# Scans and maxima with one operand in PSUM, and a reordered tail, in a two-layer graph network kernel

## The chip, the cores and the metric

The kernel runs on one core of one Trainium2 chip. The metric is device microseconds of one execution; the median of several runs counts. All inputs start in HBM and the result has to be back there.

## The reference

A graph of N = 6250 nodes with 128 features and E = 100000 edges, sorted by destination. Two layers, each followed by a residual and a layernorm. The first layer sums messages `relu(W·[x[src], edge])` per destination. The second, which the change touches, is an attention layer with 4 heads of 32 channels:

```python
xl = (x @ w_l + b_l).reshape(N, H, C)
xr = (x @ w_r + b_r).reshape(N, H, C)
e = leaky_relu(xl[src] + xr[dst], 0.2)          # every node has an edge to itself too
logits = einsum('ehc,hc->eh', e, att)
m = segment_max(logits, dst, num_segments=N)
ex = exp(logits - m[dst])
alpha = ex / segment_sum(ex, dst)[dst]
out = segment_sum(xl[src] * alpha[:, :, None], dst).reshape(N, H * C) + bias
out = (out - out.mean()) / (out.std() + 1e-5)   # over the whole array
x = layernorm(x + out * ln_w + ln_b)
```

## The kernel before

**Tiling.** Nodes lie in 49 blocks of 128. Edges lie in 784 tiles of 128, four tiles (512 edges) to a group, GN = 196 groups. The program runs in stages: node projections and index tables; layer 1 over the groups; layer 2 over the groups (1321 to 2697 us of the profile); a final stage with the global mean and deviation and the last layernorm, seven groups of BG = 7 blocks each, about 38 us. A second version of the layers, `far`, is for graphs that are not sorted well enough and is not entered here.

**Layer 2** is one loop over steps s, its order written out by hand, with no scheduler. A step issues, in this order:

- `gather_group(s + 4)`: four indirect DMAs by GpSimd (L262), each 128 rows of `xl_t` into a ring of 30 groups (`XG`). A slot of the ring is free once `values` of its group is done.
- on SyncE's queue, `store_sums` of groups that were summed in the step before (L1005, `out_t<-win`), loads `m_load` (`dm`) and `out_load` (L1010, `s<-out_t`), and `load_rows` (`xr`, `ds`). A store adds nothing: it writes a window of 128 consecutive destination rows at a row number read at run time, and windows may overlap, so stores, and the loads of the same table, follow each other in order.
- `copy_both(s-1)` (ACT, L818, `z<-pz`), `both(s)` (PE, L811 transposes of the gathered rows and L814 the destination rows, into `pz`), `leaky(s-1)` (DVE, L821), `logits(s-2)` (PE, L840, into `plg`), `onehot_t(s+1)` (ACT, L804).
- `sums(u)` for the groups u due in step s (PE, L985: one-hot `a` times values `v`, into the window `pa`) and `keep_sums` (ACT, L1001, `win`).
- for the groups due in the next step: `values_w` (ACT, L969), `values` (DVE, L973, gathered rows times weights, into `v`), and the one-hot of destinations (DVE, L579, `a`).
- what a plan lists for that step: parts of the softmax chain and of the outputs.

**The chain.** Logits of twelve groups (a macro: 15 of twelve, then 9 and 7) stand as 48 rows (head, group) of 512 in PSUM, `plg`. One macro's chain goes through six steps: `m_logits` copies `plg` to SBUF (ACT, L857, `lg`) and makes `pen`, -BIG where a new destination starts (DVE, L860 and L861); `m_forward` and `m_back` take running maxima within a destination with scans (L865, L869); `m_ends`, `m_groups`, `m_before` carry maxima over from group to group (PE, small DVE operations on one partition, PE); `m_maxima` makes each edge's maximum `mx` from the scans and carried values (`fp` L922, L924), then `lg - mx` (L926), and ACT exponentiates; `m_weights`, `m_left`, `m_ready` turn the weights back to edges on partitions. The PSUM bank `pw` is one buffer, handed from use to use in that order. `m_logits` stands at the front of its step (list `FIRST`), the others at its end. Two groups of values are due per step from step 166 on, one before.

**Outputs.** Once all windows of a block are stored, `out_load` brings its sums back from `out_t`, `out_weights` (L1019 to L1026, the first operation writes `m0`) weighs them against the node's own edge, and `output` (L1034 to L1042) normalises them and adds the own edge. Its last part, `ready`, takes bn statistics of the block and multiplies `xl` by `ln_w` (L259). Blocks go by twos, the last few singly, and the last three (46 to 48) together. Load, weights and output are planned 1, 4 and 5 steps after the step in which the last store's group is summed.

The head of the loop shows how gathers, stores and the front of the plan stand to each other:

```python
for s in range(stop + 1):
    if s + AHEAD < GN:
        gather_group(s + AHEAD, xl_t)
    for u in due.get(s - 1, ()):
        store_sums(u)
    planned(s, only=FIRST)
```

Of the kernel before, what the change touches and what calls it, by code (L numbers as in the profile page):

```python
# [9 lines left out]
F32 = mybir.dt.float32  # L10
# [72 lines left out]
def gnn_resnorm(  # L83
# [165 lines left out]
    def ready(pool, b0, n):  # L249


        bs = slice(b0, b0 + n)
        st = pool.tile([P, n, nc.vector.BN_STATS_DIM], F32, name=f"rd_st{n}")
        for b in range(n + 1):
            if b < n:
                nc.vector.bn_stats(st[:, b, :], xl[:, b0 + b, :])
            if b > 0:
                nc.vector.bn_aggr(stat[:, b0 + b - 1, :], st[:, b - 1, :])
        nc.vector.tensor_tensor(xl[:, bs, :], xl[:, bs, :], over(lnw_b, n), op=OP.mult)  # L259
# [294 lines left out]
    def near():  # L554
        ctx = ExitStack()
        with ctx:
# [24 lines left out]

            def first_row(g):
# [192 lines left out]
            with tc.tile_pool(name="e1", bufs=3) as pool, tc.tile_pool(name="e1m", bufs=2) as mp, \  # L775
# [79 lines left out]
                def m_logits(m):  # L855
                    m.lg = mp.tile([m.R, S], F32, name="lg")
                    nc.scalar.copy(m.lg, m.plg)  # L857
# [5 lines left out]
                def m_forward(m):  # L863
                    m.fw = mp.tile([m.R, S], F32, name="fw", bufs=1)
                    nc.vector.tensor_tensor_scan(m.fw, m.pen[:, 0:S], m.lg, -BIG, op0=OP.add, op1=OP.max)  # L865

                def m_back(m):
                    m.sm = mp.tile([m.R, S], F32, name="sm", bufs=1)
                    nc.vector.tensor_tensor_scan(m.sm[:, ::-1], m.pen[:, S:0:-1], m.fw[:, ::-1], -BIG,  # L869
                                                 op0=OP.add, op1=OP.max)  # L870

                    m.ends = mp.tile([m.R, 2], F32, name="ends")
# [5 lines left out]
                def m_ends(m):  # L878
                    m.pe = ps1.tile([P, S], F32, name="pw")
                    for i, t in enumerate((m.ends[:, 0:1], m.fw[:, S - 1:S], m.ends[:, 1:2], m.sm[:, 0:1])):  # L880
# [32 lines left out]
                def m_maxima(m):  # L913
# [4 lines left out]
                    m.mx = mp.tile([R, S], F32, name="mx")  # L918
                    for k, most in ((0, m.sm), (1, m.mx)):
                        fp = mp.tile([R, S], F32, name="fp", bufs=1)  # L920
# [5 lines left out]
                    nc.vector.tensor_sub(m.lg, m.lg, m.mx)  # L926
# [86 lines left out]
                def out_weights(b0, n):  # L1013
# [5 lines left out]
                    nc.vector.tensor_scalar(m0, s[:, :, :, 0], 0.5, -BIG, op0=OP.is_lt, op1=OP.mult)  # L1019
                    nc.vector.tensor_add(m0, m0, s[:, :, :, 1])  # L1020
                    mm = pool.tile([P, n, H], F32, name=f"mm{n}")
                    nc.vector.tensor_tensor(mm, lself[:, bs, :], m0, op=OP.max)
                    f = pool.tile([P, 2, n, H], F32, name=f"f{n}")
# [3 lines left out]
                    OUTS[b0] = s, f  # L1027

                def output(b0, n):
# [4 lines left out]
                    nc.vector.tensor_tensor(den, s[:, :, :, 0], f[:, 0], op=OP.mult)  # L1034
                    nc.vector.tensor_add(den, den, f[:, 1])
                    nc.vector.reciprocal(den, den)
                    nc.vector.tensor_tensor(f, f, den.unsqueeze(1).to_broadcast([P, 2, n, H]), op=OP.mult)
                    xh = xl[:, bs, :].rearrange("p b (h c) -> p b h c", h=H)
# [4 lines left out]
                    ready(pool, b0, n)  # L1043
# [10 lines left out]
                def planned(s, only=None, but=()):  # L1054
                    for f, of_what in at.get(s, ()):
                        if f not in but and (only is None or f in only):
                            f(*of_what)

# [18 lines left out]
                stop = max(when.values())  # L1077
                b = 0
                while b < NB - last:
                    n = 2 if b + 2 <= NB - last - 4 else 1  # L1080
                    s = when[FINAL[b + n - 1]] + 1
                    for i, f in ((1, out_load), (4, out_weights), (5, output)):
                        plan(s + i, f, b, n)
                    stop = max(stop, s + 5)
                    b += n
                stop += 1
                for i, f in enumerate((out_load, out_weights, output)):
                    plan(when[GN - 1] + 1 if i == 0 else stop, f, NB - last, last)
# [7 lines left out]
                FIRST = (m_load, out_load, m_logits)  # L1096
                for s in range(stop + 1):
# [20 lines left out]
                    for u in due.get(s + 1, ()):  # L1118
                        values_w(u)
                        values(u)  # L1120
                        OH[u] = onehot(pool, u, F32)
                    planned(s, but=FIRST)
# [285 lines left out]
```

## Time and profile before

| | us |
|---|---|
| median of 7 runs (lowest to highest) | 2748.42 (2733.93 to 2757.9) |
| the profiled execution's own time | 2737.26 |
| its span, first to last instruction | 2735.5 |
| GpSimd busy (1574 instructions) | 1507.8, 55% |
| PE busy (6269) | 1538.9, 56% |
| VectorE busy (2990) | 1216.9, 44% |
| ACT busy (1543) | 691.9, 25% |
| mean granted TensorE clock | 0.739 of full speed |

Busy time counts an engine's instructions only, not the issuing of DMAs nor waits. Shares are means over stages that have different limits; GpSimd's 782 gathers of layer 2 (`ring<-xl_t`) and 722 of layer 1 are nearly all of its time. Rows of the costliest groups read: line, engine, operation, result and operands, how many, then busy us and mean ns of one, then idle time just ahead of them and what ended most of it. In a timeline a row is start, duration, engine, line, operation, and in brackets the idle time ahead of it and what ended it.

### The profile page before, as it was taken

What the parts mean: (1) busy time and instruction counts of PE and PEld (TensorE: products, weight loads), DVE (VectorE), ACT (ScalarE), POOL (GpSimd) and SP (SyncE); (2) the same over time, 40 slices, a digit from 0 to 9 for tenths busy, and PEclk for the clock granted to TensorE, in tenths of its full rate; (3) what the DMA queues carried; (4) which work ended last, traced back from release to release, by engine and by line L of the source; (5) the groups of instructions that cost most, each with busy time, mean ns of one, the idle gap of its engine ahead of it and who ended that gap; (6) DMA issues with size and microseconds to landing.
All of it is one profiled execution on the core that took longest, in us unless ns stands there. A gap on an engine that the chain in (4) does not pass through costs nothing. (4 is left out here: it accounts for less than half of the span.)

```text
span 2735.5 us, 23587 instructions
## 1 busy us (share of the span) xinstructions
PE 1538.9 (56%) x6269; PEld 932.7 (34%) x6269; DVE 1216.9 (44%) x2990; ACT 691.9 (25%) x1543; POOL 1507.8 (55%) x1574
## 2 busy tenths in 40 slices
PE   2423544434444544467423877776777776766684
PEld 1223433333333333345101333333333333333342
DVE  2401343334444445489201534453444454455488
ACT  0101211111111111122102423333333333333333
POOL 7175666666666666620573566666665565664300
PEclk7666766676676677778656877887877787888787
DMA  4231333333333233332322323332333333333212
GB/s 116 79 82 49 70 73 71 77 70 77 76 83 81 70 87 85 85 79 62 93 61 63 100 77 95 94 98 89 91 99 89 92 104 92 98 97 92 84 43 62
DMA packets 252495, 224.66 MB, mean 82 GB/s; under 512 B 134793, under 2 KB 213751, under 8 KB 252354
## 3 DMA queue, kind: packets, MB, share of 16 engines
q1 hardware_dynamic: 201088, 120.00, 15.4%
q0 software_dynamic: 50048, 102.60, 14.9%
q8 instruction: 53, 0.87, 0.1%
q14 instruction: 88, 0.72, 0.1%
q10 hardware_dynamic: 1218, 0.47, 0.1%
HBM read 198.37 MB, written 24.56 MB: 81 GB/s over the span
## 5 line engine op out<-in xcount | busy, mean ns | idle before, releaser
L262 POOL DMA_INDIRECT ring<-xl_t,src_i x782 | 762.9, 976 | 612.8 <-issue 228.3
L262 POOL DMA_INDIRECT ring<-xw_t,src_i x722 | 684.1, 948 | 466.8 <-issue 195.0
L821 DVE SCALAR_TENSOR_TENSOR z<-z,pz 128x512 f32<-128x512 f32 x196 | 134.2, 685 | 677.9 <-ACT z L818 357.7
L985 PE MATMUL pa<-v,a 128*128 128x136 f32 x1568 | 280.1, 322 | 160.2 <-issue 81.3
L616 PE MATMUL pt<-ident,ef 128*128 128x128 f32 x392 | 102.0, 352 | 452.2 <-ACT fT L620 269.2
L985 PEld LDWEIGHTS pa<-v,a 128*128 128x128 f32 x1568 | 230.8, 216 | 333.7 <-issue 212.9
L579 DVE TENSOR_TENSOR a<-rows_q,dl 128x512 fp32r<-128x512 f32 (+1 forms) x392 | 267.0, 681 | 22.2 <-remote 17.7
L635 PE MATMUL ph<-wc,fT 128*128 128x256 f32 x784 | 267.3, 475 | 7.2 <-DVE msg L653 7.2
L653 DVE SCALAR_TENSOR_TENSOR msg<-ph,msg 128x512 fp32r<-128x512 f32 x196 | 134.8, 688 | 298.2 <-ACT msg L649 209.3
L814 PE MATMUL pz<-ds,xr 128*128 128x512 f32 x392 | 248.5, 720 | 3.6 <-issue 3.4
L840 PE MATMUL plg<-z,attw 128*48 128x512 f32 (+2 forms) x392 | 240.9, 696 | 13.3 <-issue 13.1
L811 PE MATMUL pz<-ident,ring 128*128 128x128 f32 x784 | 152.9, 323 | 151.7 <-issue 108.9
L616 PEld LDWEIGHTS pt<-ident,ef 128*128 128x128 f32 x392 | 60.4, 176 | 506.8 <-ACT fT L620 291.2
L818 ACT COPY z<-pz 128x512 f32<-128x512 f32 x196 | 114.2, 583 | 393.1 <-remote 230.3
L649 ACT ACTIVATE msg<-ph 128x512 fp32r<-128x512 f32 x196 | 117.6, 600 | 353.6 <-remote 160.3
L644 DVE TENSOR_TENSOR ph<-ph,ring 128x512 f32<-128x512 f32 x181 | 125.7, 695 | 175.4 <-remote 151.5
L620 ACT COPY fT<-pt 128x256 f32<-128x256 f32 x196 | 72.6, 370 | 484.1 <-remote 364.5
L635 PEld LDWEIGHTS ph<-wc,fT 128*128 128x128 f32 x784 | 174.1, 243 | 45.3 <-issue 11.7
L663 PE MATMUL pa<-msg,a 128*128 128x258 f32 x784 | 183.6, 369 | 0.0
L811 PEld LDWEIGHTS pz<-ident,ring 128*128 128x128 f32 x784 | 101.8, 161 | 201.3 <-issue 145.0
L973 DVE TENSOR_TENSOR v<-ring,rows_q 128x512 f32<-128x512 f32 x196 | 133.1, 679 | 59.2 <-remote 53.1
L804 ACT ACTIVATE ds<-ds,nb 128x512 f32<-128x512 f32 x196 | 142.4, 727 | 12.3 <-DMA ds<-dpad 12.3
(219 smaller groups left out, 1614.7 us busy)
## 6 DMA issues: line engine op xcount, KB each, us to landing
ds<-dpad SPq DMA_DIRECT2D x98, 512.0 KB
ef<-in_edge_attr_dram SPq DMA_DIRECT2D x48, 512.0 KB
ring<-xl_t,src_i POOLq DMA_INDIRECT x782
ring<-xw_t,src_i POOLq DMA_INDIRECT x722
out_t<-win SPq DMA_DIRECT2D x81, 68.0 KB
sum_t<-win SPq DMA_DIRECT2D x81, 64.5 KB
xr<-xr_t SPq DMA_DIRECT2D x81, 64.0 KB
xw_t<-xw SPq DMA_DIRECT2D x7, 448.0 KB
```

The lines of the kernel that those rows point to most:

```text
L262: nc.gpsimd.indirect_dma_start(out=to, out_offset=None, in_=table[0:min(table.shape[0], NP), :], in_offset=bass.IndirectOffsetOnAxis(ap=in ...
L579: nc.vector.tensor_tensor(a, over(iota_q, G), spread(dl[:, g * G:(g + 1) * G], W), op=OP.is_equal)
L616: nc.tensor.transpose(pt[:, g % 2, i, :], EF[c][:, o + 2 * i:o + 2 * i + 2, :], ident)
L635: nc.tensor.matmul(ph[:, 2 * i:2 * i + 2, :], fT[:, i, :], wc, start=i == 0 or g >= RAW, stop=g >= RAW, skip_group_check=g < RAW)
L653: nc.vector.scalar_tensor_tensor(msg[:, :, 1, 0:D], PH.pop(g), 0.0, msg[:, :, 0, 0:D].bitcast(F32), op0=OP.max, op1=OP.subtract)
L663: nc.tensor.matmul(pa, a[:, j, :], msgs[g % 3][:, j], start=g == o and j == 0, stop=j == G - 1, skip_group_check=True)
L804: nc.scalar.activation(DS[g], DS[g], AF.Abs, bias=nb[0:W, g:g + 1])
L811: nc.tensor.matmul(pz[:, j * P:(j + 1) * P], XG[g][:, j, :], ident, is_transpose=True, start=j == 0, stop=False, skip_group_check=True)
L814: nc.tensor.matmul(pz, xr, DS.pop(g), start=False, stop=True, skip_group_check=True)
L821: nc.vector.scalar_tensor_tensor(Z[g], Z[g], SLOPE, PZ.pop(g), op0=OP.mult, op1=OP.max)
L840: nc.tensor.matmul(m.plg, attw[m.mg][:, m.mg - i:m.mg - i + m.R], Z.pop(g), start=i == 0, stop=i == m.mg - 1)
L985: nc.tensor.matmul(pa, a[:, j, :], v[:, j].rearrange("p h c -> p (h c)"), start=u == o and j == 0, stop=j == G - 1, skip_group_check=True)
```

## The change

- `m_logits` no longer copies the logits to SBUF; the forward scan reads `plg` in PSUM. `m_logits` (now only `pen`) leaves `FIRST` and stands at the end of its step.
- The forward scan writes the PSUM bank `pw` (as `m.q`), the back scan reads it there; its last column is copied to a third column of `ends` for PE.
- `fp` lies in a bank `pw` of PSUM too, and `lg` is now `plg - mx`.
- For steps s from 192 (`late`, the last gather is issued in 191) the order within a step changes: the chain first, then `values_w` of all groups due, then on GpSimd the one-hots of every second group due a step later (`onehot_g`, eight groups in all, four 128x128 instructions each, a tile of its own with two buffers), then values, VectorE's one-hots and parts of the outputs in turn. `out_weights` and `output` become generators for that.
- The outputs of blocks from `LATE` = 34 on are planned at 1, 2 and 2 steps after their last sum instead of 1, 4 and 5, and not before step 192; the loop ends at step 210 instead of 213.
- The products by `ln_w` of blocks 34 to 48 leave `ready`; GpSimd makes them after the loop in three instructions (1, 7 and 7 blocks).

```diff
@@ -246,7 +246,7 @@
         nc.vector.tensor_tensor(y, y, over(att_b, n), op=OP.mult)
         nc.vector.tensor_reduce(lself[:, bs, :], y.rearrange("p b (h c) -> p b h c", h=H), AX.X, OP.add)
 
-    def ready(pool, b0, n):
+    def ready(pool, b0, n, scaled=True):
 
 
         bs = slice(b0, b0 + n)
@@ -256,7 +256,8 @@
                 nc.vector.bn_stats(st[:, b, :], xl[:, b0 + b, :])
             if b > 0:
                 nc.vector.bn_aggr(stat[:, b0 + b - 1, :], st[:, b - 1, :])
-        nc.vector.tensor_tensor(xl[:, bs, :], xl[:, bs, :], over(lnw_b, n), op=OP.mult)
+        if scaled:
+            nc.vector.tensor_tensor(xl[:, bs, :], xl[:, bs, :], over(lnw_b, n), op=OP.mult)
 
     def gather(to, table, index, t):
         nc.gpsimd.indirect_dma_start(
@@ -579,6 +580,13 @@
                 nc.vector.tensor_tensor(a, over(iota_q, G), spread(dl[:, g * G:(g + 1) * G], W), op=OP.is_equal)
                 return a
 
+            def onehot_g(pool, g):
+
+                a = pool.tile([P, G, W], F32, name="b", bufs=2)
+                for j in range(G):
+                    nc.gpsimd.tensor_scalar(a[:, j, :], iota_w, dl[:, g * G + j:g * G + j + 1], None, op0=OP.is_equal)
+                return a
+
             def first_row(g):
                 return nc.values_load(fst[0:1, g:g + 1], engines=(SP,), min_val=0, max_val=N - 1,
                                       skip_runtime_bounds_check_because="a destination, from 0 to N - 1")
@@ -853,23 +861,22 @@
 
 
                 def m_logits(m):
-                    m.lg = mp.tile([m.R, S], F32, name="lg")
-                    nc.scalar.copy(m.lg, m.plg)
 
                     m.pen = mp.tile([m.R, S + 1], F32, name="pen")
                     nc.vector.tensor_tensor(m.pen, m.dm[:, 1:], m.dm[:, 0:S + 1], op=OP.not_equal)
                     nc.vector.tensor_scalar(m.pen, m.pen, -BIG, None, op0=OP.mult)
 
                 def m_forward(m):
-                    m.fw = mp.tile([m.R, S], F32, name="fw", bufs=1)
-                    nc.vector.tensor_tensor_scan(m.fw, m.pen[:, 0:S], m.lg, -BIG, op0=OP.add, op1=OP.max)
+                    m.q = ps1.tile([P, S], F32, name="pw")[0:m.R, :]
+                    nc.vector.tensor_tensor_scan(m.q, m.pen[:, 0:S], m.plg, -BIG, op0=OP.add, op1=OP.max)
 
                 def m_back(m):
                     m.sm = mp.tile([m.R, S], F32, name="sm", bufs=1)
-                    nc.vector.tensor_tensor_scan(m.sm[:, ::-1], m.pen[:, S:0:-1], m.fw[:, ::-1], -BIG,
+                    nc.vector.tensor_tensor_scan(m.sm[:, ::-1], m.pen[:, S:0:-1], m.q[:, ::-1], -BIG,
                                                  op0=OP.add, op1=OP.max)
 
-                    m.ends = mp.tile([m.R, 2], F32, name="ends")
+                    m.ends = mp.tile([m.R, 3], F32, name="ends")
+                    nc.vector.tensor_copy(m.ends[:, 2:3], m.q[:, S - 1:S])
                     nc.vector.tensor_scalar(m.ends[:, 0:1], m.dm[:, S:S + 1], m.dm[:, 0:1], -BIG,
                                             op0=OP.not_equal, op1=OP.mult)
                     nc.vector.tensor_scalar(m.ends[:, 1:2], m.dm[:, 1:2], m.dm[:, S + 1:S + 2], -BIG,
@@ -877,7 +884,7 @@
 
                 def m_ends(m):
                     m.pe = ps1.tile([P, S], F32, name="pw")
-                    for i, t in enumerate((m.ends[:, 0:1], m.fw[:, S - 1:S], m.ends[:, 1:2], m.sm[:, 0:1])):
+                    for i, t in enumerate((m.ends[:, 0:1], m.ends[:, 2:3], m.ends[:, 1:2], m.sm[:, 0:1])):
                         nc.tensor.transpose(m.pe[0:1, i * P:i * P + m.R], t, ident[0:m.R, 0:m.R])
 
                 def m_groups(m):
@@ -916,14 +923,15 @@
                     nc.vector.tensor_copy(prev, m.pv[0:R, 0:2])
 
                     m.mx = mp.tile([R, S], F32, name="mx")
+                    fp = ps1.tile([P, S], F32, name="pw")[0:R, :]
                     for k, most in ((0, m.sm), (1, m.mx)):
-                        fp = mp.tile([R, S], F32, name="fp", bufs=1)
                         o = k * (S + 1)
                         nc.vector.tensor_scalar(fp, m.dm[:, 1:S + 1], m.dm[:, o:o + 1], -BIG,
                                                 op0=OP.not_equal, op1=OP.mult)
                         nc.vector.scalar_tensor_tensor(m.mx, fp, prev[:, k:k + 1], most, op0=OP.add, op1=OP.max)
 
-                    nc.vector.tensor_sub(m.lg, m.lg, m.mx)
+                    m.lg = mp.tile([R, S], F32, name="lg")
+                    nc.vector.tensor_sub(m.lg, m.plg, m.mx)
                     m.sc = mp.tile([R, 1], F32, name="sc")
                     nc.vector.scalar_tensor_tensor(m.sc, m.pen[:, 0:1], prev[:, 0:1], m.mx[:, 0:1], op0=OP.add,
                                                    op1=OP.subtract)
@@ -1017,14 +1025,18 @@
 
                     m0 = pool.tile([P, n, H], F32, name=f"m0{n}")
                     nc.vector.tensor_scalar(m0, s[:, :, :, 0], 0.5, -BIG, op0=OP.is_lt, op1=OP.mult)
+                    yield
                     nc.vector.tensor_add(m0, m0, s[:, :, :, 1])
+                    yield
                     mm = pool.tile([P, n, H], F32, name=f"mm{n}")
                     nc.vector.tensor_tensor(mm, lself[:, bs, :], m0, op=OP.max)
+                    yield
                     f = pool.tile([P, 2, n, H], F32, name=f"f{n}")
                     nc.vector.tensor_sub(f[:, 0], m0, mm)
                     nc.vector.tensor_sub(f[:, 1], lself[:, bs, :], mm)
                     nc.scalar.activation(f, f, AF.Exp)
                     OUTS[b0] = s, f
+                    yield
 
                 def output(b0, n):
 
@@ -1032,15 +1044,20 @@
                     s, f = OUTS.pop(b0)
                     den = pool.tile([P, n, H], F32, name=f"den{n}")
                     nc.vector.tensor_tensor(den, s[:, :, :, 0], f[:, 0], op=OP.mult)
+                    yield
                     nc.vector.tensor_add(den, den, f[:, 1])
+                    yield
                     nc.vector.reciprocal(den, den)
+                    yield
                     nc.vector.tensor_tensor(f, f, den.unsqueeze(1).to_broadcast([P, 2, n, H]), op=OP.mult)
+                    yield
                     xh = xl[:, bs, :].rearrange("p b (h c) -> p b h c", h=H)
                     sh = s[:, :, :, 2:]
                     nc.vector.tensor_tensor(sh, sh, f[:, 0].unsqueeze(3).to_broadcast([P, n, H, C]), op=OP.mult)
                     nc.vector.tensor_tensor(xh, xh, f[:, 1].unsqueeze(3).to_broadcast([P, n, H, C]), op=OP.mult)
                     nc.vector.tensor_add(xh, xh, sh)
-                    ready(pool, b0, n)
+                    yield
+                    ready(pool, b0, n, b0 < LATE)
                     if b0 == NB - last:
                         root = pool.tile([1, 1], F32, name="root")
                         nc.scalar.activation(root, ones[0:1, 0:1], AF.Sqrt)
@@ -1055,6 +1072,12 @@
                     for f, of_what in at.get(s, ()):
                         if f not in but and (only is None or f in only):
                             f(*of_what)
+
+                def planned_outputs(s):
+
+                    for f, of_what in at.get(s, ()):
+                        if f in OUTPUTS:
+                            yield from f(*of_what)
 
                 when, busy = {}, {}
                 begin = []
@@ -1074,18 +1097,22 @@
                 due = {}
                 for u in range(GN):
                     due.setdefault(when[u], []).append(u)
-                stop = max(when.values())
+                stop = max(when.values()) + 2
+                OUTPUTS = (out_weights, output)
+                late = GN - AHEAD
+                LATE = None
                 b = 0
                 while b < NB - last:
                     n = 2 if b + 2 <= NB - last - 4 else 1
                     s = when[FINAL[b + n - 1]] + 1
-                    for i, f in ((1, out_load), (4, out_weights), (5, output)):
-                        plan(s + i, f, b, n)
-                    stop = max(stop, s + 5)
+                    if LATE is None and s + 5 >= late:
+                        LATE = b
+                    for i, f in ((1, out_load), (4, out_weights), (5, output)) if b != LATE and LATE is None else                             ((1, out_load), (2, out_weights), (2, output)):
+                        plan(max(s + i, late) if LATE is not None and f in OUTPUTS else s + i, f, b, n)
                     b += n
-                stop += 1
                 for i, f in enumerate((out_load, out_weights, output)):
-                    plan(when[GN - 1] + 1 if i == 0 else stop, f, NB - last, last)
+                    plan(stop - (i == 0), f, NB - last, last)
+                CHAIN = sum(M_STEPS, ())
                 early = 4
                 assert GN % 2 == 0
                 for g in range(early):
@@ -1093,7 +1120,7 @@
                 for g in range(AHEAD):
                     gather_group(g, xl_t)
                 onehot_t(0)
-                FIRST = (m_load, out_load, m_logits)
+                FIRST = (m_load, out_load)
                 for s in range(stop + 1):
                     if s + AHEAD < GN:
                         gather_group(s + AHEAD, xl_t)
@@ -1115,11 +1142,34 @@
                     for u in due.get(s, ()):
                         sums(u)
                         keep_sums(u)
-                    for u in due.get(s + 1, ()):
+                    us = due.get(s + 1, ())
+                    if s < late:
+                        for u in us:
+                            values_w(u)
+                            values(u)
+                            OH[u] = onehot(pool, u, F32)
+                        planned(s, only=CHAIN, but=FIRST)
+                        for _ in planned_outputs(s):
+                            pass
+                        continue
+                    planned(s, only=CHAIN, but=FIRST)
+                    for u in us:
                         values_w(u)
+                    for u in due.get(s + 2, ())[1:]:
+                        OH[u] = onehot_g(pool, u)
+                    outs = planned_outputs(s)
+                    for i, u in enumerate(us):
                         values(u)
-                        OH[u] = onehot(pool, u, F32)
-                    planned(s, but=FIRST)
+                        for _ in range(1 if i else 4):
+                            next(outs, None)
+                        if u not in OH:
+                            OH[u] = onehot(pool, u, F32)
+                            next(outs, None)
+                    for _ in outs:
+                        pass
+                for b in sorted({LATE, *range(-(-LATE // BG) * BG, NB, BG)}):
+                    e = min((b // BG + 1) * BG, NB)
+                    nc.gpsimd.tensor_tensor(xl[:, b:e, :], xl[:, b:e, :], over(lnw_b, e - b), op=OP.mult)
 
             final()
```

## Prediction

> **What bounds it now.** I began with the page's busy shares and its costliest groups, then cut the span into stages with the windows view, and read the second graph layer (1321 to 2697 us), the only stage the change touches, instruction by instruction in the timelines of GpSimd, VectorE and SyncE. In the windows view the columns are the stretch, its length, and busy us (instructions) of PE, weight loads, DVE, ACT and POOL, then clock, DMA share and GB/s.
>
> ```profile
> L262 POOL DMA_INDIRECT ring<-xl_t,src_i x782 | 762.9, 976 | 612.8 <-issue 228.3
> 1534.00:2440.00 906.00, 654.47 (x2580) 335.64 (x2580) 414.78 (x969) 321.33 (x686) 567.20 (x576) 0.80 0.32 94
> 2440.00:2613.00 173.00, 115.98 (x490) 59.62 (x490) 92.23 (x243) 59.89 (x139) 70.77 (x74) 0.80 0.29 87
> 2613.00:2666.00 53.00, 40.30 (x213) 24.89 (x212) 44.69 (x136) 15.00 (x49) 0.00 (x0) 0.87 0.12 32
> 2666.00:2697.00 31.00, 17.94 (x86) 11.98 (x86) 27.82 (x113) 6.24 (x24) 0.00 (x0) 0.83 0.12 32
> ```
>
> There are two regimes. Up to the last gather (2609.7) GpSimd is the fullest engine: 576 gathers of 0.97 us plus the 0.30 us it needs between two make 740 of the 906 us. After it GpSimd is idle, and VectorE is: 44.7 of 53, then 27.8 of 31 us.
>
> The gathers of the steady stretch, and the DVE instruction beside one of them (start, duration):
>
> ```profile
> 1606.05 0.95 POOL L262 DMA_INDIRECT ring<-xl_t,src_i  x1 [0.30 <-issue]
> 1612.04 0.94 POOL L262 DMA_INDIRECT ring<-xl_t,src_i  x1 [5.04 <-PE pz L811]
> ...
> 1620.79 0.95 POOL L262 DMA_INDIRECT ring<-xl_t,src_i  x1 [0.30 <-PE pz L811]
> 1622.04 1.93 POOL L262 DMA_INDIRECT ring<-xl_t,src_i  x1 [0.30 <-issue]
> 1624.27 0.95 POOL L262 DMA_INDIRECT ring<-xl_t,src_i  x1 [0.30 <-issue]
> ```
> ```profile
> 1622.00 1.21 DVE L865 TENSOR_TENSOR_SCAN fw<-pen,lg 48x512 f32<-48x512 f32 x1
> ```
>
> A gather takes 0.95 us, but the one that starts beside the forward scan takes 1.93: it is held until the scan ends. Between runs of 8 to 24 gathers GpSimd stands still for about 5 us (44 stalls, 163 us in this stretch), when its ring of 30 groups is full. Such a stall ends with a value product (L973), which frees a slot. Before most of the long ones ACT and PE had been nearly idle, and came back only 2 to 3 us after the last gather had ended (ACT at 1609.39, the gather at 1607.00). I read a period as "a run of gathers, then a fixed 5 us", so that what a gather loses the stage loses.
>
> **Part one: scans and maxima with an operand in PSUM.** I summed every gather's time above 0.95 us over the stage: 23.6 us. Of it 13.7 us are in gathers that overlap a scan (L865, L869), 2.2 us in those that overlap fp, mx or lg (L922, L924, L926), and 7.7 beside instructions that keep both operands in SBUF (L860, L949, the outputs). The trace has no scan with an operand in PSUM, so I bound it: the nearest rows are L973 (ring and the PSUM rows) and L821 (z and pz), one operand in each memory, which run once a step and beside which alone no gather grew. At best all 15.9 us go; at worst none. I take -14, by those two rows, leaving 2 us for other instructions in the same overlaps.
>
> [...]
>
> What the change costs VectorE: fp (L922) takes 0.478 us from SBUF to SBUF, and L926, the same 48x512, takes 0.683 with two operands. With fp in PSUM I bound it by 0.478 and 0.683 and take the upper end: 34 x 0.2 = 7 us of VectorE. A new 48-row copy is 17 x 0.15 = 2.6 us (as L916, 0.14). In the gather stage VectorE is busy 415 of 906 us and hides them; only the last two chains (4 fp, 2 copies, 1.1 us) lie in the tail. [...]
>
> The copy of the logits leaves ACT (L857, 17 x 0.58), and the two pen instructions (L860 0.67, L861 0.43) move from the front of their step to its end. All three stood ahead of the z copy, leaky and value product that a stall waits for. Stalls end in about one step of four or five (44 in 143 steps), so 17 chains meet some 4, at 0.6 to 1.7 us: 0 to -6, I take -2.
>
> The bank pw is now also written by VectorE (forward scan, fp); each such write stands between PE's uses of that bank in the same chain, where PE waited for a later VectorE result anyway. I cost it at nothing; uncovered it would be the scan's 1.2 us per chain, 20 us.
>
> **Part two: the tail, 2613 to 2697.** Eight of the one-hots (L579, 0.60 start to start) go to GpSimd, five before the last chain's first value product (2666.20), three after: -3.0 and -1.8 us of VectorE. The multiplication by ln_w of blocks 34 to 48 (L259: 0.31 for two blocks, 0.18 for one, 0.5 for three) goes to GpSimd: -0.9 before 2666.20. But the outputs of blocks 40 to 42 now stand before that product: 3.4 and 2.6 us more, with the chain's 1.1. Net +3.2 us of VectorE in a stretch of which it idles 8.3; I take +0.5 (0 to +3.2).
>
> From there SyncE's queue sets the end:
>
> ```profile
> 2670.66 7.64 SPq L1005 DMA_DIRECT2D out_t<-win  x4
> 2679.56 0.34 SPq L1010 DMA_DIRECT2D s<-out_t  x1
> 2681.49 2.03 SPq L1005 DMA_DIRECT2D out_t<-win  x2
> 2684.83 0.34 SPq L1010 DMA_DIRECT2D s<-out_t  x1
> 2686.74 0.33 SPq L1005 DMA_DIRECT2D out_t<-win  x1
> 2688.33 0.40 SPq L1010 DMA_DIRECT2D s<-out_t  x1
> ```
>
> Each store and load waits for the one before it to land (1.6 to 1.9 us apart), so from the third store (2676) on the sequence runs at its own pace, and its order stays. It can start earlier: the third value product stands 3.4 us behind the first (2669.57), after two one-hots and the weights of block 40, and ACT's exponential of the next weights held the third window's copy until 2675.95. With GpSimd's one-hots and block 40 gone that is 2.1 us and no such hold-up: I take -3.5 (0 to -5). The last three blocks' ln_w (L259, 0.5 us) leaves the end: -0.5.
>
> GpSimd's price is in no row: a one-hot is four 128x128 instructions, between the 0.23 us of an IOTA of that size and a gather's 0.95, so 0.9 to 3.8 us. It is issued a step earlier than VectorE's was, with steps of 4 to 6 us, so it is covered; beyond about 6 us PE's sums (L985) would wait for it. Its SBUF reads can hold VectorE's outputs as the scans held gathers: 0 to +5 us, I take +0.5. GpSimd's three ln_w products (128, 896 and 896 elements) are needed from group 4 of the final stage on (2716.70), 20 us after the last output; a VectorE product of 896 takes 1.1 us, and even ten times that is covered. [...]
>
> **Sum.** -14 - 2 + 0.5 - 3.5 - 0.5 + 0.5 = -19 on the profiled execution (2737.3: span 2735.5 and 1.8 around it), so 2718. That execution lay 11 us below the median of the seven (2748.4), so I forecast 2729.
>
> **Rivals.**
> The loop is paced by the engines. PE is busy 654 of 906 us, more than GpSimd without its gaps, and gathers are 8 to 10 groups ahead of the step. Then shorter gathers only lengthen the 5 us stalls, and the tail's -3 remains: 2745. For it: before 1472 steps came every 22.4 us although GpSimd never stood still. Against it: the stalls are alike after runs of very different length.
> The change does not do what it says: a scan with one operand in PSUM still holds the gather, as its other operand and its result are in SBUF. Also 2745, -2 left of part one.
> Slower: outputs wait on VectorE for their own loads. Load and weights were three steps apart and are now one; behind the waiting m (L1019) queue the value products and one-hots of the next step, and PE's sums behind those. From the last window's copy (2683.43) to the first operation on its load (2691.72) are 8.3 us; store, load and use now lie two steps apart, 8 us at steps of 4 us. It decides once steps fall under 4 us. If each of nine outputs lost one step's cover, 4 us, that is +36; with -16 from part one, 2768.
>
> **Numbers.** Differences within 0.5% (14 us) are about what a measurement of this kernel can't tell from no change; that begins at 2735. Forecast 0.58, of which 0.10 lies above 2735 because part of the gather time turns into stall; the two rivals at 2745 together 0.30, of which 0.03 below 2735; slower 0.12, 0.01 of it within the bound. So faster 0.51, same 0.38, slower 0.11. Range: low end all 15.9, -6 and -5 and some spread between runs, 2709; high end beyond 2745 by that spread and the lesser waits of outputs, 2756.
>
> **What would show it.** Gathers beside the scans at 0.95 us, and the sum above 0.95 down from 23.6 to about 9; stalls still near 5 us and not more of them (if they grow by what the gathers gain, the first rival holds); the last gather some 16 us earlier; from the last gather to the final stage 84 us instead of 87; no idle time ahead of m in the tail (else the third rival). It is wrong if the gathers shorten and the last one does not come earlier.

## The result and the profile after

The changed kernel takes 2770.58 us (median of 15 runs), the kernel before 2748.30 (36 runs): a ratio of 1.0069, 95% interval 1.0050 to 1.0089. It is 22 us slower, where 19 us faster were forecast. The profiled execution of after took 2764.82 us (span 2763.1), that of before 2737.26 (span 2735.5).

The runs of this study fell on different chips, and they are of two kinds. On some the kernel before takes 2748 to 2777 us, on others 2133 to 2135. I call them stalling and free chips, for a reason that the traces show below. Each chip of the experiments was met in one session only, so whether the kind belongs to the chip or to its state at the time isn't shown. The record, and both profiles of it, come from stalling chips. Ratios are always to the kernel before on the same chip.

First the gathers of layer 2 among the costliest groups of after's page (busy us, mean ns of one, then idle time ahead of them and what ended most of it):

```profile
L263 POOL DMA_INDIRECT ring<-xl_t,src_i x782 | 745.8, 954 | 649.6 <-issue 249.2
```

Before had 762.9, 976 and 612.8. The gathers became 17.1 us shorter, as the forecast wanted, but GpSimd's idle time grew by 36.8. After's timeline of GpSimd and VectorE at a forward scan shows why they became shorter:

```profile
1553.48 0.94 POOL L263 DMA_INDIRECT ring<-xl_t,src_i  x1 [0.30 <-issue]
1554.04 1.22 DVE L871 TENSOR_TENSOR_SCAN pw<-pen,plg 48x512 f32<-48x512 f32 x1
1554.73 0.94 POOL L263 DMA_INDIRECT ring<-xl_t,src_i  x1 [0.30 <-PE plg L848]
```

A gather that starts within the scan now takes 0.94 us instead of 1.93. In after none of the 26 gathers that start within one of the two scans takes over 0.95 us; in before 19 of 26 take 1.03 to 1.93. Over the stage the sum above 0.95 us a gather fell from 23.6 to 7.8.

The stages of after in the windows view (stretch, length, busy us of PE, weight loads, DVE, ACT, POOL, then clock, DMA share, GB/s); the last three are the tail from the last gather to the first value product of the last macro, from there to the final stage, and the final stage:

```profile
1534.00:2440.00 906.00, 644.85 (x2561) 329.04 (x2562) 421.50 (x976) 313.09 (x670) 542.33 (x568) 0.80 0.32 93
2629.50:2690.60 61.10, 45.81 (x239) 28.27 (x237) 51.67 (x166) 16.79 (x58) 16.71 (x28) 0.79 0.13 35
2690.60:2722.10 31.50, 19.32 (x82) 12.92 (x82) 20.98 (x73) 4.80 (x18) 4.99 (x7) 0.77 0.10 27
2722.10:2763.10 41.00, 13.13 (x40) 8.77 (x40) 30.91 (x146) 19.37 (x54) 1.87 (x1) 0.67 0.29 81
```

The same three stretches of the tail of before:

```profile
2609.70:2666.20 56.50, 43.60 (x234) 26.91 (x232) 47.60 (x141) 16.41 (x54) 0.00 (x0) 0.87 0.13 36
2666.20:2696.70 30.50, 17.94 (x86) 11.98 (x86) 27.39 (x111) 6.18 (x24) 0.00 (x0) 0.84 0.12 33
2696.70:2735.50 38.80, 13.16 (x40) 8.82 (x40) 29.27 (x147) 19.14 (x54) 0.00 (x0) 0.68 0.30 85
```

So the 27.6 us between the two spans lie here: from the first gather to the last 1308.3 instead of 1288.6 us (+19.7: gathers -17.1, stalls of GpSimd +38.2, from 303.5 us in 52 stalls to 341.7 in 57, the regular gaps -1.4); from the last gather to the final stage 92.6 instead of 87.0 (+5.6); final stage +2.2. In the steady stretch after makes 568 gathers in the time of 576.

Where a longer stall comes from is seen in one of 10 us, in after's timeline:

```profile
2182.26 0.94 POOL L263 DMA_INDIRECT ring<-xl_t,src_i  x1 [0.30 <-issue]
2185.95 0.15 DVE L923 COPY prev<-pw 48x2 f32<-48x2 f32 x1 [11.66 <-remote]
2186.14 0.75 DVE L929 TENSOR_SCALAR pw<-dm 48x512 f32<-48x512 f32 x1
...
2186.92 0.74 DVE L931 SCALAR_TENSOR_TENSOR mx<-pw,prev,sm 48x512 f32<-48x512 f32 x1
...
2187.70 0.75 DVE L929 TENSOR_SCALAR pw<-dm 48x512 f32<-48x512 f32 x1
...
2188.48 0.74 DVE L931 SCALAR_TENSOR_TENSOR mx<-pw,prev,mx 48x512 f32<-48x512 f32 x1
...
2189.25 0.68 DVE L934 TENSOR_TENSOR lg<-plg,mx 48x512 f32<-48x512 f32 x1
...
2191.19 0.69 DVE L829 SCALAR_TENSOR_TENSOR z<-z,pz 128x512 f32<-128x512 f32 x1 [1.13 <-ACT z L826]
2191.80 0.68 DVE L981 TENSOR_TENSOR v<-ring,rows_q 128x512 f32<-128x512 f32 x1
...
2193.22 1.41 POOL L263 DMA_INDIRECT ring<-xl_t,src_i  x1 [10.01 <-issue]
```

The ring is full, GpSimd waits. VectorE had waited 11.66 us for two columns from PE, and gets them 2.75 us after the last gather has ended. Then it does the whole of m_maxima, 4.1 us (2185.95 to 2190.06), and only behind that the leaky and the value product (L981) that frees a slot: it ends at 2192.48, and the next gather starts 0.74 us later, as after a value product in 47 of the 57 stalls. From this stall I estimate that a chain step between the end of the wait and the value product can cost GpSimd up to its full length.

Three stalls of each trace are longer; together they grew by 6.6 us. Summed over all stalls of under 11 us, VectorE's time inside them divides like this (worked out from the traces):

| us inside GpSimd's stalls | before | after |
|---|---|---|
| all of them (number) | 192.3 (49) | 223.9 (54) |
| softmax chain | 7.9 | 18.4 |
| leaky, values, one-hots | 83.8 | 96.1 |
| outputs | 2.6 | 5.7 |
| VectorE idle | 98.0 | 103.7 |

Of the 31.6 us by which these stalls grew, the chain makes 10.5. The leaky, values and one-hots make 12.3 (there are five more stalls), outputs 3.1, and VectorE's idle time 5.7.

Such waits for PE tell the two kinds of chips apart. In the timeline of before, on the stalling chip of the record:

```profile
1598.26 1.02 PE L814 MATMUL pz<-ds,xr 128*128 128x512 f32 x2
...
1606.05 0.95 POOL L262 DMA_INDIRECT ring<-xl_t,src_i  x1 [0.30 <-issue]
...
1609.39 0.59 ACT L818 COPY z<-pz 128x512 f32<-128x512 f32 x1 [10.84 <-remote]
```

PE's product ends at 1599.28 by the model; ACT, which waits for nothing else, copies it 10.1 us later, 2.4 us after the last gather of that run has ended. The releaser reads "remote" because no instruction ended near the moment at which the signal arrived. The trace's semaphore events agree: a signal of PE is recorded at 1609.36, 0.03 us ahead of the copy, as one of fourteen within 0.6 us. Of PE's 1217 recorded signals in the gather stage, 381 come within 0.06 us of the one before; on a free chip (before_here, below) it is 12 of 1498. There no wait of the gather stage is ended by "remote", and GpSimd doesn't stall at all. As PE's ends are modelled, the trace can't tell a late signal from a product that itself ended late.

Two more things differ between the kinds. The granted clock in the gather stage is 0.78 in before and 0.94 in before_here. And the record of the stalling chips has holes: before's trace holds 1874 of VectorE's 2790 signals and 957 of ACT's 1501, before_here's 2784 and 1501. Whether the recording itself takes part in the delays is a rival that no run here tests.

### The profile page after: what moved, and what is told of

The parts are those of the page before. It is cut to its first block, busy times and chain, and to the rows that moved or that the text cites. A ratio compares the mean times of both kernels' runs of the same rounds, so it can differ in the third digit from the quotient of the medians.

```text
span 2763.1 us, 23628 instructions
## 1 busy us (share of the span) xinstructions
PE 1543.2 (56%) x6269; PEld 930.8 (34%) x6269; DVE 1225.1 (44%) x2990; ACT 682.6 (25%) x1526; POOL 1513.4 (55%) x1609
## 5 line engine op out<-in xcount | busy, mean ns | idle before, releaser
L263 POOL DMA_INDIRECT ring<-xl_t,src_i x782 | 745.8, 954 | 649.6 <-issue 249.2
L993 PE MATMUL pa<-v,a 128*128 128x136 f32 x1504 | 265.9, 319 | 152.3 <-ACT v L977 73.6
L993 PEld LDWEIGHTS pa<-v,a 128*128 128x128 f32 x1504 | 217.6, 212 | 325.0 <-issue 187.6
L580 DVE TENSOR_TENSOR a<-rows_q,dl 128x512 fp32r<-128x512 f32 (+1 forms) x384 | 261.3, 680 | 36.9 <-remote 35.1
L981 DVE TENSOR_TENSOR v<-ring,rows_q 128x512 f32<-128x512 f32 x196 | 132.8, 678 | 55.4 <-remote 42.3
L812 ACT ACTIVATE ds<-ds,nb 128x512 f32<-128x512 f32 x196 | 142.3, 726 | 12.3 <-DMA ds<-dpad 12.3
```

The source lines that it names most:

```text
L263: nc.gpsimd.indirect_dma_start(out=to, out_offset=None, in_=table[0:min(table.shape[0], NP), :], in_offset=bass.IndirectOffsetOnAxis(ap=in ...
L580: nc.vector.tensor_tensor(a, over(iota_q, G), spread(dl[:, g * G:(g + 1) * G], W), op=OP.is_equal)
L812: nc.scalar.activation(DS[g], DS[g], AF.Abs, bias=nb[0:W, g:g + 1])
L993: nc.tensor.matmul(pa, a[:, j, :], v[:, j].rearrange("p h c -> p (h c)"), start=u == o and j == 0, stop=j == G - 1, skip_group_check=True)
```

## The experiments

Theory A says that the loop is paced by engines whose chain the change has lengthened; theory B that the tail alone costs; theory C, formed when the first runs had fallen on a free chip, that the sign depends on whether GpSimd's gathers follow one another without a stall; theory D that it is the same everywhere.

### Each part alone, on a free chip

Part one alone takes all of the diff's `m_` functions and `FIRST`, and the loop's tail of before. Storage alone keeps ACT's copy and the place of `m_logits`; no copy alone keeps fw and fp in SBUF. The tail alone keeps the chain of before and needs room for GpSimd's one-hots:

```diff
-                        fp = mp.tile([R, S], F32, name="fp", bufs=1)
+                        fp = mp.tile([R, S], F32, name="fw", bufs=1)
```

> Part one alone (PSUM operands, no logits copy, pen at the end of its step; the tail as before). Theory A, the loop is paced by the engines' own chain and VectorE's longer chain lies on it: gathers shorten as in the changed kernel (sum above 0.95 us near 8), yet the last gather comes 10 to 20 us later than before and the time is 2755 to 2770. Theory B, the loop's loss in the one profile is spread between executions and the tail alone costs: 2735 to 2750.

> Part two alone (order from step 192, GpSimd's one-hots and ln_w products, outputs at 1, 2 and 2 steps; fp shares fw's SBUF buffer to make room for GpSimd's one-hots; the chain's storage as before). Theory A: the last gather as before within a few us, last gather to the end 4 to 8 us longer, 2752 to 2757. Theory B: all of the loss, 2765 to 2772.

> Scan result and fp in PSUM alone; the copy of the logits by ACT and the place of pen as before, the tail as before. Theory A (VectorE's 7 us for fp in PSUM and 2.6 us of copies are on the loop's path): 2755 to 2765. If the loss of part one comes from moving pen and dropping the copy instead: 2740 to 2750.

> No copy of the logits and pen at the end of its step, storage of scan result and fp in SBUF as before, the tail as before. Theory A: 2742 to 2750, as ACT gains 10 us that nothing waits for. If the move is what costs: 2755 to 2770.

Measured, against 2133.16: part one 2120.19 (0.9940, 0.9924 to 0.9955), tail 2140.68 (1.0030, 1.0020 to 1.0041), storage 2125.27 (0.9962, 0.9947 to 0.9977), no copy 2126.81 (0.9973, 0.9962 to 0.9983). The times expected were those of a stalling chip, so none could be met. Part one gains 13 us, and each of its halves gains alone (storage 7.9, no copy 6.4); the tail costs 7.5. In none of the four traces has GpSimd a stall in layer 2: 782 gathers and their gaps fill the stage, so what the gathers lose the stage loses. The rows of part one and, from a later run, of before on a free chip:

```profile
L262 POOL DMA_INDIRECT ring<-xl_t,src_i x782 | 744.2, 952 | 273.3 <-issue 90.5 <-DMA ring<-xl_t,src_i 65.2 <-DMA xr_t<-r 35.3
```
```profile
L262 POOL DMA_INDIRECT ring<-xl_t,src_i x782 | 759.2, 971 | 273.8 <-issue 122.2 <-DMA xr_t<-r 35.8 <-PE pz L811 32.6
```

Idle time is the same 273 us (of it 238 are the regular gaps), and the 15.0 us between the gathers' sums are the gain: the stage takes 982.2 instead of 997.2 us. No copy alone, whose forward scan reads the logits in PSUM, shortens gathers too (748.9 us in all).

### The whole, more gathers and less work for PE, on a stalling chip

```diff
@@ more gathers: beside gather_group(s + AHEAD, xl_t)
+                        if s % 2:
+                            gather(pool.tile([P, D], F32, name="spare", bufs=2), xl_t, src_i, (s + AHEAD) * G)
@@ less PE: logits(g)
+                    if i % 2 == 0:
                         nc.tensor.matmul(m.plg, ...)
```

> The whole change once more, beside its parts, on whichever chip these runs get. Theory C: the sign depends on whether GpSimd's gathers are the bound. On a chip where they follow one another without a stall (before near 2133 us, granted clock 0.84) parts add up: -0.6% for part one and +0.3% for the tail, -4 to -8 us against before. On a chip where the loop stalls GpSimd (before near 2748 us, clock 0.74): +15 to +25 us. Theory D: the sign is that of the change, and the whole is slower by 10 us or more everywhere.

> Before, with one gather more in every second step of layer 2, into a spare tile that nothing reads: 96 gathers of 1.25 us, 120 us of GpSimd. Theory C: on a chip where GpSimd never stalls +110 to +125 us; where it stalls for 163 of 906 us, 0 to +60 us. If gathers bound the loop everywhere (the record's step): +110 to +125 on either.

> Before, with the logits matmul of every second group left out (PE does 98 x 1.04 = 102 us less; the logits are incomplete). Theory C: on a chip where GpSimd never stalls 0 to -5 us; where it stalls, PE's own speed paces the loop, -40 to -100 us. If the loop there waits for something other than PE: 0 to -15 us.

Against 2770.55: the whole 2794.21 (1.0084, 1.0057 to 1.0111), so the loss is real and repeats, with stalls of 356.7 us and 133.3 us from the last gather to the end (after's own 133.6, before's 125.8). More gathers: 2913.10 (1.0521, 1.0496 to 1.0546), +142.5 us or 1.48 for each of the 96; far over the 0 to 60 of theory C, above the 110 to 125 of its rival too, and more than the 1.25 us that each lasts with its gap. Less work for PE: 2756.07 (0.9945, 0.9928 to 0.9962), -14.5, where 102 us of PE are gone; PE's own speed does not pace the loop there, as the range of 0 to -15 said for that case. The 300 us of stalls are no slack: a gather more costs more than itself.

### Parts and old distances, on another stalling chip

Old distances is the whole change with one edit:

```diff
-... if b != LATE and LATE is None else ((1, out_load), (2, out_weights), (2, output)):
+... if True else ():                       # (1, out_load), (4, out_weights), (5, output)
-                stop = max(when.values()) + 2
+                stop = max(when.values()) + 5
```

and the last three blocks' load again one step after the last sum.

> Part one alone again, wanted on a chip where before takes about 2750 us. Theory C (there, what the gathers gain goes into more and longer stalls of GpSimd, because PE's signals come through only when gathers pause, and VectorE's longer chain stands between that and the next free slot): +8 to +20 us against before, sum of the stalls 20 to 40 us above before's 303. Theory E (part one is neutral there, the whole loss is the tail's): -5 to +5. On a chip where GpSimd never stalls: -0.6% again.

> Scan result and fp in PSUM, with ACT's copy of the logits and pen's place as before. If the longer VectorE chain (fp 0.75 for 0.47 us, one copy more) is what lengthens the stalls where GpSimd stalls: +8 to +20 us. If the moved pen and the dropped copy are: -5 to +5. Without stalls: -0.4% again.

> No copy of the logits, pen at the end of its step, storage as before. If moving pen behind the value product is what lengthens the stalls where GpSimd stalls: +8 to +20 us. Otherwise -8 to +3. Without stalls: -0.3% again.

> The whole change, but outputs keep their distances of 1, 4 and 5 steps (the loop ends at step 213 again). If outputs waiting for their loads and for ACT's exponential are what the tail loses, it is 4 to 6 us faster than the whole change on the same chip, and from the last gather to the end takes 127 to 130 us where the whole takes 133. If the chain put first and GpSimd's products are: within 2 us of the whole change.

Against 2769.04: part one 2781.88 (1.0043, 1.0023 to 1.0062), storage 2781.62 (1.0054, 1.0032 to 1.0076), no copy 2775.70 (1.0021, 1.0002 to 1.0040), old distances 2780.52 (1.0044, 1.0023 to 1.0064). Part one loses 13 us here, as theory C expected, with stalls of 348 us, and storage in PSUM does so by itself: VectorE's chain inside the stalls is about 21 us with storage and 18 with part one, but 9 with no copy (before's trace: 8). No copy's 6.7 us lie between its two ranges, and their interval hardly excludes nothing. Old distances equals part one: from the last gather to the end it takes 125.7 us, part one 127.2, so with the old distances the rest of the tail costs nothing in sum. It reaches the final stage 84.8 us after the last gather (part one 88.4) and loses 2.1 of this in the final stage. The whole change was not run on this chip; on the others of its kind that end took 133.3 and 133.6 us.

### Gathers or GpSimd's time? A larger ring, fp in SBUF

```diff
@@ GpSimd's work: beside gather_group(s + AHEAD, xl_t)
+                        if s % 2:
+                            spare = pool.tile([P, D], F32, name="spare", bufs=2)
+                            for _ in range(2):
+                                nc.gpsimd.tensor_scalar(spare, iota_w, dl[:, 0:1], None, op0=OP.is_equal)
@@ fp in SBUF, in part one
-                    fp = ps1.tile([P, S], F32, name="pw")[0:R, :]
+                        fp = mp.tile([R, S], F32, name="fp", bufs=1)
@@ ring of 31, in before
-BUFS = 30
+BUFS = 31
```

> The kernel before once more, for its trace on the chip of these runs. Where it takes about 2750 to 2770 us: some 50 stalls of GpSimd in layer 2, 300 to 320 us together, and near 8 us of VectorE's chain within them. Where it takes about 2133: none.

> Before, with two 128x128 products of GpSimd into a spare tile in every second step of layer 2 (about 1.17 us, as long as the extra gather of the run with more gathers cost, 96 times, 112 us in all; nothing reads them). If it is running gathers that hold the other engines up, these leave them free and come out of the 300 us of stalls: 0 to +50 us where GpSimd stalls. If GpSimd's time as such bounds the loop: +110 to +145, like the extra gathers. Where GpSimd never stalls: +105 to +115.

> Part one alone, with fp kept in SBUF (only the scan's result in PSUM). If fp's 0.28 us more, 34 times, falls into the stalls: 5 to 10 us faster than part one, 2 to +6 against before where GpSimd stalls. If the scan's result in PSUM brings the loss: within 3 us of part one, +9 to +15 against before. Where GpSimd never stalls: within 2 us of part one's -0.6%.

> Before, with a ring of 31 groups for 30. If a stall costs a fixed time and its number falls with the room in the ring: -5 to -25 us where GpSimd stalls. If engines and gathers take turns and the ring only shifts them: -5 to +3. Where GpSimd never stalls: -2 to +2.

They fell on a free chip. Before's trace there has no stall. GpSimd's work cost 127.5 us against 2134.54 (1.0599, 1.0583 to 1.0615), a little over the range given: two products and their gaps take 1.33 us. fp in SBUF gave 0.9945 (0.9931 to 0.9959), not to be told from part one's 0.9940: on a free chip VectorE's longer fp is hidden. The ring of 31 gave 0.9988 (0.9977 to 0.9999), -2.9 us for an expected -2 to +2. What the last two do on a stalling chip was not measured.

> As before: two 128x128 products of GpSimd in every second step of layer 2, which nothing reads. Where GpSimd never stalls they cost 127 us, 1.33 us each pair. Where it stalls: 0 to +60 us if only running gathers hold the other engines up, +110 to +145 if GpSimd's time as such bounds the loop, as 96 extra gathers did (+142).

> The whole change. Where GpSimd never stalls: part one's -13 us and the tail's +7.5 add up to -4 to -8 us against before. Where it stalls: +18 to +25 us again.

A free chip again: GpSimd's work +130.1 (1.0616), the whole change 2126.59 against 2133.43 (0.9972, 0.9961 to 0.9984). -6.8 us, near the -5.5 of its parts: on a free chip the change is faster, and part one alone is the better kernel (0.9940).

> The same two products of GpSimd in every second step, once more. Where GpSimd stalls: 0 to +60 us if only running gathers hold the other engines up (the products then fall into the 300 us of stalls), +110 to +145 if GpSimd's time as such bounds the loop. Where it never stalls: +127 again.

This one fell on a stalling chip: 2726.31 against 2777.02, a ratio of 0.9820 (0.9801 to 0.9838). 123 us more work for GpSimd make the kernel 50.7 us faster, outside both ranges. GpSimd's rows in the groups of that trace:

```profile
L262 POOL DMA_INDIRECT ring<-xl_t,src_i x782 | 766.5, 980 | 443.0 <-issue 191.2 <-PE pz L811 122.8 <-DMA xr_t<-r 86.9
...
L1103 POOL TENSOR_SCALAR spare<-iota_w,dl 128x128 f32<-128x128 f32 x192 | 123.4, 642 | 12.0
```

GpSimd is busy 889.8 us in the stage instead of 762.9, but it stalls 17 times for 135.1 us, instead of 52 times for 303.5 in the record's before. The stage takes 1257.9 us, in the record's before 1288.6. 96 more gathers cost 142 us on one stalling chip, 96 pairs of products, about as long each, gain 51 on another. That speaks for running gathers, and not GpSimd's time, as what keeps the other engines waiting on these chips, and for a pause between gathers as what lets them go on; the mechanism was not shown.

## Why the prediction was wrong, step by step

**What bounds the kernel.** The step that failed is the reading of a period as "a run of gathers, then a fixed 5 us", by which what a gather loses the stage loses. On a free chip that rule is exact for the stage (15.0 us for 15.0), but the profile read was of a chip on which it is not: gathers lost 17.1 us and the stage grew by 19.7, as the stalls grew by 38.2. The 5 us are not fixed: the stalls last 5.8 us in the mean in before and 6.0 in after, and those of under 11 us run from 0.5 to 6.4 and from 0.7 to 10.0. The one of 10 us lasts until VectorE's wait for PE ends, 2.75 us after the last gather, and VectorE reaches the next value product, with whatever stands ahead of it in its queue. The observation that ACT and PE come back 2 to 3 us after the last gather was in the prediction, as a detail of the wait; the late start is a part of the wait itself.

**Part one, -14 and -2.** The first term's size was right: gathers beside scans take 0.94 us, the sum above 0.95 went to 7.8 where 9 was said (15.8 gone of the bound of 15.9), and on a free chip part one gains 13 us. On the record's chip the last gather came 19.8 us later instead of 16 earlier. The second term, the dropped copy and moved pen, was never run by itself: no copy, -6 us on a free chip and +7 on a stalling one, also holds the forward scan's shorter gathers. Its working has a slip too, as 44 stalls in 143 steps are one in about three, not in four or five.

**VectorE's price "hidden by the gather stage".** fp cost 0.75 us, above the 0.683 taken as its upper end: 34 x 0.27 = 9.1 us. That 415 of 906 us were busy was taken as cover. It is cover on a free chip (0.9940 with fp in PSUM, 0.9945 in SBUF); on a stalling one the chain in the stalls grew by 10.5 us, which stands there ahead of the product that frees a slot. How much of it is fp's length and how much the moment at which chain steps fall is open, as fp in SBUF was run on a free chip alone. Why storage in PSUM moves more of the chain into the stalls, and why there are more stalls, is open too.

**The tail, -3.5, -0.5 and +0.5 each.** This was wrong on both kinds of chips: from the last gather to the final stage 92.6 us instead of 84, and the tail alone costs 7.5 us on a free chip. Up to the last chain's first value product it lost 4.6 us where +0.5 was said, from there to the final stage 1.0 where -4 was said. VectorE does wait in the outputs, not ahead of m for a load (0.20 us once) but ahead of den for ACT's exponential, as out_weights and output now stand in one step. First a den of before, straight behind its weights, then after's timeline:

```profile
2682.49 0.21 ACT L1026 ACTIVATE f<-f 128x8 f32<-128x8 f32 x1 [1.88 <-DVE f L1025]
2682.73 0.16 DVE L1034 TENSOR_TENSOR den<-s,f 128x4 f32<-128x4 f32 x1 [0.28 <-ACT f L1026]
```
```profile
2694.74 0.27 ACT L1009 COPY win<-pa 128x136 f32<-128x136 f32 x1 [6.05 <-PE pa L1003]
2696.76 0.27 ACT L1009 COPY win<-pa 128x136 f32<-128x136 f32 x1 [1.75 <-PE pa L1003]
2697.24 0.21 ACT L1037 ACTIVATE f<-f 128x8 f32<-128x8 f32 x1
2697.49 0.16 DVE L1046 TENSOR_TENSOR den<-s,f 128x4 f32<-128x4 f32 x1 [2.88 <-ACT f L1037]
...
2698.80 2.49 POOL L1172 TENSOR_TENSOR xl<-xl,row_ln_w 128x128 f32<-128x128 f32 x2
...
2699.31 2.13 DVE L1056 TENSOR_TENSOR s<-s,f 128x128 f32<-128x128 f32 x1
...
2711.83 0.16 DVE L1046 TENSOR_TENSOR den<-s,f 128x4 f32<-128x4 f32 x1 [5.47 <-ACT f L1037]
...
2721.90 2.07 POOL L1172 TENSOR_TENSOR xl<-xl,row_ln_w 128x896 f32<-128x896 f32 x1 [20.61 <-DVE stat L258]
2722.07 1.92 DVE L470 TENSOR_SCALAR stat<-stat,valid 128x2 f32<-128x2 f32 x1
2724.28 0.20 DVE L480 TENSOR_REDUCE one<-stat 128x1 f32<-128x49 f32 x1 [0.28 <-DVE stat L470]
```

The exponential stands in ACT's queue behind the window copies, and those behind PE's sums; VectorE's next value products stand behind den. Eight such waits come to 12.3 us, the longest 5.47; before has four, 1.1 us together. The old distances leave three, 0.8 us together, and reach the final stage after 84.8 us. That is near the 84 forecast, but by luck, as the forecast counted on the new distances. The term that was put at nothing is the wait for the exponential when output stands in the step of its weights.

**"Even ten times that is covered".** GpSimd's one-hots took 2.33 to 2.71 us, inside the bounds of 0.9 to 3.8. Its last ln_w product took 2.07 us, far below ten times VectorE's 1.1. The product is not needed for 20 us, but it is not free: it started 0.17 us ahead of VectorE's first operation of the final stage, which took 1.92 us, and the next one starts 2.21 us behind it. In before:

```profile
2696.74 0.22 DVE L469 TENSOR_SCALAR stat<-stat,valid 128x2 f32<-128x2 f32 x1
2697.15 0.20 DVE L479 TENSOR_REDUCE one<-stat 128x1 f32<-128x49 f32 x1 [0.19 <-issue]
```

That is +1.8 us on the path. The other full product, issued at 2699.22 within the merged row above, runs beside an output of VectorE (L1056) that takes 2.13 us; the same shape takes 0.29 elsewhere. Together that is some 3.5 us against the +0.5 (0 to +5) put down for outputs that GpSimd holds up. The cover was counted for who waits for the result, and hardly for who stands beside the instruction. In each of the two full products one VectorE instruction started, and it ended just behind the product: L470 at 2723.99 and the product at 2723.97, L1056 at 2701.44 and the product at 2701.29. That its reads would hold VectorE was the prediction's estimate; what held it here was not shown.

**The rivals.** The first (shorter gathers only lengthen the stalls) was the nearest, and its sign of trouble, steps of 22.4 us while GpSimd never stood still, was in the text; but it held the gain for the most that stalls could take back. They took back 38 for 17. The second is refuted: a scan with one operand in PSUM does not hold a gather (0.95 us at most in the 26 of after). Its own time is 2743 by the prediction's terms, not 2745. The third, slower, had the right sign and place, but it named the wait for the loads where ACT's exponential was waited for, and put it at 36 us where the old distances give back some 8.

## What to carry to other kernels

A long idle time of an engine is no cover until its end is explained: find the event that ends it, and count all that stands in the queue between that event and the instruction that frees the resource. An operation moved to an idle engine still has neighbours: look at what runs beside it in the first microseconds (here 1.92 us for an operation that took 0.22 in before), not only at when its result is due. And profile on more than one chip where runs of one program differ as these do (2133 and 2748 us): a change can gain on one and lose on the other, for reasons that one trace cannot show.

## What the runs showed of the hardware

The same program takes 2133 us on some chips and 2748 to 2777 on others, at a mean granted clock of 0.84 and 0.74. The difference lies in both layers: before's first gather of layer 2 starts at 1022.0 and 1321.1 us, and the gather stage takes 997.2 and 1288.6. On the slower chips the engines that wait for PE were let go as much as 10.1 us after the modelled end of its product, 2.4 us after a run of indirect DMAs, and 381 of 1217 recorded signals of PE came within 0.06 us of another. That 96 pairs of products of GpSimd, which nothing reads, gain 51 us there, where 96 more gathers cost 142, speaks for the pauses; what holds PE's results or signals back, and why on some chips alone, stays open. A kernel with part one, old distances and such pauses was not run.
